# A recurrent step on four TensorE column tiles: seven equal x products a step instead of eight unequal ones, and a VectorE wait moved to a memset

## The chip, the cores and the metric

The kernel runs on one core of a Trainium2 chip. The metric is the device time of one execution in microseconds. Before the change the median of three runs is 1675.38 us (1673.64 to 1677.71).

## The reference, cut to what matters

Eight sequences of 512 steps and 512 features go through a gated recurrent cell with 512 units; the result is added to the input.

```python
def step(h, x_t):
    fused = sigmoid(concat([x_t, h], -1) @ w_W + w_b)
    hidden_state, output_state = split(fused, 2, -1)          # r and z
    memory_state = x_t @ wx_W + wx_b + hidden_state * (h @ wh_W + wh_b)
    h_new = output_state * h + (1 - output_state) * tanh(memory_state)
    return h_new, h_new
# x: (8, 512, 512) float32; out = x + all h_new
```

A step needs h times three 512 x 512 matrices (for r, for z and for hh, the product that r scales), and x times three. The x part does not depend on the state and can be worked ahead. Everything is float32.

## The kernel before

**Layout.** The state lies with its units on the partitions, in four chunks of 128 (k = 0 to 3). Chunks 0 and 1 are half A (tiles `hTA`), 2 and 3 half B (`hTB`). A matmul takes a chunk of the state as its stationary operand: 32 columns wide, four time steps by eight sequences, of which the current step's eight count. The moving operand is a block of weights. The array is used as four column tiles of 32 columns; tile j (j = 0 to 3) writes PSUM partitions 32j to 32j+31, and each tile has its own quarter of the weights. A float32 matmul is two weight loads and two matmul records in the profile.

**The h products of a step.** They go to three PSUM tiles: `A`, 192 columns (hh, z and r of half A), `B`, 128 (r and hh of half B) and `C`, 64 (z of half B), two of each in turn. `ORDER` (line 27) gives their order: A0 B0 A1 A2 A3 B1 B2 B3 C0 C1 C2 C3, letter and chunk; each entry is four matmuls, one per column tile, j = 0, 1, 2, 3. So the new state of half A is needed first, at A0, that of half B at A2.

**The x products.** They are worked for two groups of four steps at once, in a scheme with seven products where a plain one has eight: `products(o)` (line 289) yields their matmuls one by one, each product with two chunks k and four tiles j, on sums of weights (`tw`, lines 267 to 276) and sums of inputs (`sx`, made on GpSimd by `x_sum`). They add into four regions of two PSUM tiles `xp` (`AL`, `BE`, `GA`, `DE`, lines 35 and 36). ScalarE and VectorE copy and add these regions between steps (lines 463 to 501), at fixed places in a group of eight steps, and `spread` (line 247) puts the results into A, B and C as starting values of a later step. Of the 14 pairs of a product and a chunk in `products`, two are cut in two halves of 96 columns, so that eight steps have 64 matmuls. After each step's h products `take(later, 8)` (line 355) issues the next eight. This holds from step 5 on; the steps before take them from `first`, and the last ones have none left.

**The elementwise chain of a step.** The order is written out by hand (line 180 turns the scheduler off, and each engine works its instructions in program order). VectorE transposes r of half A from PSUM (`tr`, line 377), then hh of half A (`md1A`, line 393), then z (`tz`). ScalarE takes the sigmoids (`act`, line 214). A VectorE scan (`scan`, line 361) computes r times hh plus the x part into `m`, ScalarE takes tanh, and a second scan (`update`) makes the new state. The two scans of a half run chunk by chunk. Half B follows in the same way between half A's instructions. The scan into `m` reads md1A, which VectorE has written itself, and md0A, which ScalarE has written; line 403 makes tz of half A, which stands before the scan, wait for md1A's transpose.

**The step's end.** After the copies, three memsets of one column of the tile `idle` (line 506) stand on VectorE ahead of the next step's tr. GpSimd adds the input to the state for the output, and SyncE stores 16 steps at a time.

Of the kernel before, what the change touches and what calls it, by code (L numbers as in the profile page):

```python
# [14 lines left out]
NQ = 4  # L15
# [7 lines left out]
IDLE = 3  # L23
# [9 lines left out]
HALF = 192  # L33
# [8 lines left out]
def tile_cond_rnn_residual(  # L42
# [39 lines left out]
    nc = tc.nc  # L82
# [51 lines left out]
    def wh(bank, k, j):  # L134
        return wa[:, k, j] if bank == "A" else wb[:, k, j, {"C": slice(0, 64), "B": slice(64, 192)}[bank]]
# [30 lines left out]
    idle = const.tile([P, IDLE], F32, name="idle")  # L166
# [8 lines left out]
    def state(hf, i, slot=2):  # L175

        s = i % GS
        return hT[hf][i % NH][:, B * s : B * s + B, :, slot]
# [8 lines left out]
    def mm(out_, lhsT, rhs, start=False):  # L187
        nc.tensor.matmul(  # L188
            out_, lhsT, rhs, start=start, stop=False, skip_group_check=True
        )  # L190
# [13 lines left out]
    for hf in range(2):  # L204
        for slot in (0, 2):
            nc.vector.tensor_copy(
                state(hf, 0, slot), hin[:, 2 * hf : 2 * hf + 2].rearrange("p c b -> p b c")
            )

# [2 lines left out]
    def act(key, out_, in_, func, **kw):  # L214
        inst = nc.scalar.activation(out_, in_, func, **kw).ins  # L215
        if key in written:
            tc.declare_no_dep(inst, written[key], reason="ordered through VectorE")
        written[key] = inst
        return inst
# [37 lines left out]
    def reg(r):  # L257
        return xps[r[0]][:, r[1]]

    def wx_of(kh, ch):  # L260
        return wx[:, 2 * kh : 2 * kh + 2, :, HALF * ch : HALF * ch + HALF]

    def x_half(o, n, kh):

        return x_of(o // 2, slice(2 * kh, 2 * kh + 2), 8 * (o % 2) + GS * n, GS)
# [23 lines left out]
    def products(o):  # L289

        t_ = [q[o % 2] for q in sx]
        for n, (to, lhs, rhs) in enumerate((
            (AL, x_half(o, 0, 0), wx_of(0, 0)),
            (DE, t_[0], tw[0]),
            (BE, t_[1], tw[1]),
            (AL, x_half(o, 0, 1), wx_of(1, 0)),
            (GA, t_[2], tw[2]),
            (BE, t_[3], wx_of(1, 1)),
            (GA, x_half(o, 1, 1), tw[3]),
        )):  # L300
            for k in range(2):
                w = HALF // 2 if (2 * n + k) % 7 == 3 else HALF
                for c0 in range(0, HALF, w):
                    for j in range(NQ):
                        mm(
                            reg(to)[32 * j : 32 * j + 32, c0 : c0 + w],
                            lhs[:, k],
                            rhs[:, k, j, c0 : c0 + w],
                        )
                        yield  # L310

    def take(it, n=None):
        while n is None or n > 0:
            if next(it, it) is it:
                return
            n = None if n is None else n - 1

    def x_side():
        for o in range(2, NG // 2):
            yield from products(o)  # L320
# [4 lines left out]
    later = x_side()  # L325
# [8 lines left out]
    for i in range(T):  # L334
# [8 lines left out]
        for n in (ORDER if i else FIRST).split():  # L343
            if n == "x":
                take(first[1], 1)
                continue
            bank, k = n[0], int(n[1])
            hs = hT[k // 2][i % NH][:, :, k % 2, 2]
            for j in range(NQ):
                to = ps[bank] if i or bank != "A" else xps[0][:, XP["A"]]  # L350
                mm(to[32 * j : 32 * j + 32, :], hs, wh(bank, k, j))
        if i < 5:
            take(first[(i + 3) // 2], 2)
        else:
            take(later, 8)

        rows = slice(B * s, B * s + B)

# [16 lines left out]
        def turned(n, hf):  # L375
            t_ = work.tile([P, 2, 32], F32, tag=f"t{n}{hf}", name=f"t{n}{hf}_{i}")
            inst = nc.vector.transpose(t_.rearrange("p c n -> p (c n)"), raw[n][hf]).ins  # L377
            return t_[:, :, rows], inst
# [19 lines left out]
                tc.add_manual_dep(inst, pool_done[i + 1 - NH].name, SYNC)  # L398

        def turn_z(hf):  # L400
            tz, inst = turned("z", hf)
            if hf == 0:
                tc.add_manual_dep(inst, h_done[0].name, SYNC)
            act(
                ("zc", hf, i % 2),
                hd0[hf][i % 2][:, :, :, 2].rearrange("p n c -> p c n"),
                tz,
                AF.Sigmoid,
                scale=-1.0,
            )  # L410
# [17 lines left out]
        turn_r(0)  # L428
        turn_h(0)
        turn_z(0)  # L430
        memory(0, 0)
        memory(0, 1)
        turn_r(1)
        turn_h(1)
        update(0, 0)
        turn_z(1)
        tc.add_manual_dep(update(0, 1), r_done[1].name, SYNC)
        if i == 0:
# [64 lines left out]
            weight_sum(1 if i < 5 else 3, *divmod((i - 1) % 4, 2))  # L503
        if i == 4:
            nc.gpsimd.tensor_tensor(step_bias, bias[:, BE[1]], bias[:, AL[1]], ALU.subtract)
        for n in range(IDLE):
            nc.vector.memset(idle[:, n : n + 1], 0.0)
        def add(hf, engine):
            return engine.tensor_tensor(  # L509
# [98 lines left out]
```

## Time and profile before

| | before |
|---|---|
| median of 3 runs | 1675.38 us (1673.64 to 1677.71) |
| profiled execution | 1671.65 us, span 1669.3 us |
| granted TensorE clock | 1.00 |
| busy PE | 1655.0 us (99%), 57230 matmul records |
| busy VectorE, ScalarE, GpSimd | 1102.7, 956.9, 300.5 us |
| DMA, mean over the span | 19 GB/s |

PE is TensorE's matmuls, PEld its weight loads, DVE VectorE, ACT ScalarE, POOL GpSimd, SP SyncE. In a group's row the numbers after the bar are busy time in us and the mean duration of one in ns; after the second bar stand the idle time of the engine before these instructions and what ended it. In a timeline row the first number is the start in us from the beginning of the span, the second the duration of the row's instructions together. In the list of waits the numbers are us in total, the number of waits and the sources. The span covers all 512 steps and a prologue.

### The profile page before, as it was taken

To read this page: it belongs to the slowest core of one execution; us is meant where nothing else is said; L and a number is where in the kernel's file an instruction comes from. 1 tells how busy PE (TensorE), PEld (TensorE's weight loads), DVE (VectorE), ACT (ScalarE), POOL (GpSimd) and SP (SyncE) were. 2 spreads that over 40 slices of the span, in tenths; PEclk is the share of its full clock that TensorE was granted. 3 is DMA by queue.
4 is the path that set the end of the run, shared out by engine and by line. 5 is a ranking of instruction groups with operands and counts; after the bars stand their busy time and mean duration, and the time that the engine had idled before them with its cause. 6 is when DMAs were issued, how large, how long until landed. Compare 5 with 4: busy or idle time off the path is not lost.

```text
span 1669.3 us, 131859 instructions
## 1 busy us (share of the span) xinstructions
PE 1655.0 (99%) x57230; PEld 1504.4 (90%) x57230; DVE 1102.7 (66%) x9387; ACT 956.9 (57%) x5822; POOL 300.5 (18%) x1281
## 2 busy tenths in 40 slices
PE   8999999999999999999999999999999999999998
PEld 5999999999999999999999989999899999999997
DVE  6666666666666666666666666666666666666666
ACT  3555555555555555555555555555555555555555
POOL 1111111111111111111111111111111111111111
PEclk9999999999999999999999999999999999999999
DMA  4000000000000000000000000000000000000000
GB/s 179 17 11 12 18 18 18 17 5 18 17 18 18 5 18 18 17 17 5 18 18 17 18 17 5 18 17 17 18 5 18 17 18 18 5 17 12 11 11 11
DMA packets 11533, 31.53 MB, mean 19 GB/s; under 512 B 1220, under 2 KB 1732, under 8 KB 10824
## 3 DMA queue, kind: packets, MB, share of 16 engines
q1 hardware_dynamic: 10800, 22.94, 3.9%
q8 instruction: 448, 7.34, 1.8%
q14 instruction: 133, 1.09, 0.2%
q10 hardware_dynamic: 152, 0.16, 0.0%
HBM read 14.70 MB, written 8.39 MB: 14 GB/s over the span
## 4 chain that ended last, share of the span: by engine, by line
PE 97%; DMA 1%; DVE 1%; issue 0%; ACT 0%; SPq 0%
PE A L188 40%; PE B L188 26%; PE xp L188 18%; PE C L188 13%; DMA wb<-in_wb_dram 1%; DMA wx<-in_wx_dram 0%; DVE tr L377 0%; DVE tz L377 0%; DVE hTA L361 0%; DVE m L361 0%; DVE md1A L393 0%; DVE md1B L393 0%; ACT hTB L215 0%; ACT xp L223 0%; DVE hTB L361 0%
## 5 line engine op out<-in xcount | busy, mean ns | idle before, releaser
L188 PE MATMUL A<-wa,hTA 128*32 128x192 f32 x8176 | 536.1, 328 | 2.8 <-DVE hTA L361 2.8
L188 PE MATMUL A<-wa,hTB 128*32 128x192 f32 x8176 | 435.6, 326 | 0.1
L188 PE MATMUL B<-wb,hTA 128*32 128x128 f32 x8192 | 429.5, 273 | 0.8 <-DMA wb<-in_wb_dram 0.8
L377 DVE STREAM_TRANSPOSE tr<-A 128x64 f32<-128x64 f32 x511 | 127.7, 250 | 435.6 <-PE A L188 435.6
L509 POOL TENSOR_TENSOR ot<-xin,hTB 128x16 f32<-128x16 f32 x503 | 125.5, 250 | 1324.8 <-DVE hTB L361 1314.1
L188 PEld LDWEIGHTS B<-wb,hTA 128*32 128x32 f32 x8192 | 307.5, 122 | 37.6 <-DMA wb<-in_wb_dram 1.1
L215 ACT ACTIVATE md0A<-tr 128x16 f32<-128x16 f32 x512 | 112.7, 220 | 397.6 <-DVE tr L377 397.6
L188 PEld LDWEIGHTS A<-wa,hTB 128*32 128x32 f32 x8176 | 292.3, 122 | 45.7 <-DVE hTB L361 0.7
L188 PE MATMUL B<-wb,hTB 128*32 128x128 f32 x8192 | 327.1, 273 | 0.1
L188 PEld LDWEIGHTS A<-wa,hTA 128*32 128x32 f32 x8176 | 263.9, 123 | 37.5 <-DVE hTA L361 22.4
L188 PEld LDWEIGHTS B<-wb,hTB 128*32 128x32 f32 x8192 | 249.6, 122 | 0.3 <-DMA wb<-in_wb_dram 0.3
L361 DVE TENSOR_TENSOR_SCAN hTB<-hd0B,hTB 128x24 f32<-128x24 f32 x1024 | 157.7, 195 | 100.5 <-ACT hTB L215 100.3
L188 PE MATMUL C<-wb,hTB 128*32 128x64 f32 x8192 | 218.6, 219 | 1.0 <-issue 1.0
L188 PE MATMUL C<-wb,hTA 128*32 128x64 f32 x8192 | 217.9, 219 | 0.0
L188 PEld LDWEIGHTS C<-wb,hTA 128*32 128x32 f32 x8192 | 195.4, 122 | 0.0
L361 DVE TENSOR_TENSOR_SCAN hTA<-hd0A,hTA 128x24 f32<-128x24 f32 x1024 | 191.0, 186 | 0.0
L188 PE MATMUL xp<-tw,sx 128*32 128x192 f32 (+1 forms) x3472 | 186.1, 303 | 0.3 <-issue 0.2
L215 ACT ACTIVATE hd0B<-tz 128x16 f32<-128x16 f32 x512 | 114.9, 224 | 110.7 <-DVE tz L377 110.7
L215 ACT ACTIVATE hd0A<-tz 128x16 f32<-128x16 f32 x512 | 115.1, 225 | 101.3 <-DVE tz L377 101.3
L188 PEld LDWEIGHTS C<-wb,hTB 128*32 128x32 f32 x8192 | 167.2, 122 | 0.9 <-issue 0.8
L215 ACT ACTIVATE hTB<-hTB 128x16 f32<-128x16 f32 x512 | 120.3, 235 | 78.7 <-DVE hTB L361 63.2
L215 ACT ACTIVATE hTB<-m 128x8 f32<-128x8 f32 x1024 | 160.6, 206 | 0.0
(91 smaller groups left out, 2281.5 us busy)
## 6 DMA issues: line engine op xcount, KB each, us to landing
xin<-in_x_dram SPq DMA_DIRECT2D x31, 256.0 KB, 3.0
out_dram<-ot SPq DMA_DIRECT2D x31, 256.0 KB, 2.2
wx<-in_wx_dram SPq DMA_DIRECT2D x4, 768.0 KB, 6.8
wa<-in_wa_dram SPq DMA_DIRECT2D x4, 384.0 KB, 8.8
wb<-in_wb_dram SPq DMA_DIRECT2D x1, 1152.0 KB
wb<-in_wb_dram SPq DMA_DIRECT2D x1, 384.0 KB, 11.2
out_dram<-ot SPq DMA_DIRECT2D x1, 192.0 KB, 1.9
head<-in_xh_dram ACTq DMA_DIRECT2D x1, 144.0 KB, 4.8
```

Of the source, the lines that this page charges most:

```text
L188: nc.tensor.matmul(out_, lhsT, rhs, start=start, stop=False, skip_group_check=True)
L215: inst = nc.scalar.activation(out_, in_, func, **kw).ins
L361: return nc.vector.tensor_tensor_scan(*[t_[:, :, c_].rearrange("p n c s -> p (n c s)") for t_ in (out_, d0, d1)], 0.0, ALU.mult, ALU.add,).ins
L377: inst = nc.vector.transpose(t_.rearrange("p c n -> p (c n)"), raw[n][hf]).ins
L509: return engine.tensor_tensor(ot[:, t, 2 * hf : 2 * hf + 2, :].rearrange("p c n -> p n c"), x_of(c, slice(2 * hf, 2 * hf + 2), t, 1).rearr ...
```

## The change

Two things change. First, `products` no longer cuts two pairs in halves: all matmuls have 192 columns, 56 of them per eight steps, and a step takes seven (`take(later, 7)`). Seven is not a multiple of four, so the column tiles are taken in turn: the variable `turn` counts the x matmuls issued, and the h products of a step begin at the tile at which the x products of the step before left off. Second, the wait for md1A's transpose of half A is taken from tz and put on a memset of the last column of `idle`, which now stands between md1A's transpose and tz in VectorE's program; the step's end has two memsets left.

```diff
@@ products(o)
-        for n, (to, lhs, rhs) in enumerate((
+        for to, lhs, rhs in (
 ...
             for k in range(2):
-                w = HALF // 2 if (2 * n + k) % 7 == 3 else HALF
-                for c0 in range(0, HALF, w):
-                    for j in range(NQ):
-                        mm(
-                            reg(to)[32 * j : 32 * j + 32, c0 : c0 + w],
-                            lhs[:, k],
-                            rhs[:, k, j, c0 : c0 + w],
-                        )
-                        yield
+                for j in range(NQ):
+                    mm(reg(to)[32 * j : 32 * j + 32], lhs[:, k], rhs[:, k, j])
+                    yield
@@ the step's h products (turn = [0] before the loop)
             for j in range(NQ):
+                j = (j + turn[0]) % NQ
                 to = ps[bank] if i or bank != "A" else xps[0][:, XP["A"]]
                 mm(to[32 * j : 32 * j + 32, :], hs, wh(bank, k, j))
         if i < 5:
             take(first[(i + 3) // 2], 2)
         else:
-            take(later, 8)
+            take(later, 7)
+            turn[0] += 7
@@ turn_z(hf)
-            tz, inst = turned("z", hf)
+            tz, _ = turned("z", hf)
             if hf == 0:
+                inst = nc.vector.memset(idle[:, IDLE - 1 :], 0.0).ins
                 tc.add_manual_dep(inst, h_done[0].name, SYNC)
@@ the step's end
-        for n in range(IDLE):
+        for n in range(IDLE - 1):
             nc.vector.memset(idle[:, n : n + 1], 0.0)
```

## The prediction

> **What bounds the kernel now.** I read the page's parts 1 and 4 first, then the list of waits, then the timeline step by step.
>
> ```profile
> PE 1655.0 (99%) x57230; PEld 1504.4 (90%) x57230; DVE 1102.7 (66%) x9387; ACT 956.9 (57%) x5822; POOL 300.5 (18%) x1281
> PE 97%; DMA 1%; DVE 1%; issue 0%; ACT 0%; SPq 0%
> PEld A L188 <- DVE hTA L361: 22.4, 119, 0.4
> ```
>
> TensorE is nearly the whole chain, and the only wait of the steady state that reaches it is its first weight load of a step (bank A, stationary hTA) waiting for VectorE's new state: 22.4 us, in 119 steps. A share cannot say which steps these are. The start of the transpose `tr<-A` marks each step once; here are three stretches of the VectorE timeline.
>
> ```profile
> 802.44 0.25 DVE L377 STREAM_TRANSPOSE tr<-A 128x64 f32<-128x64 f32 x1 [0.60 <-PE A L188]
> 805.56 0.25 DVE L377 STREAM_TRANSPOSE tr<-A 128x64 f32<-128x64 f32 x1 [0.59 <-PE A L188]
> 808.83 0.25 DVE L377 STREAM_TRANSPOSE tr<-A 128x64 f32<-128x64 f32 x1 [0.97 <-PE A L188]
> 812.10 0.25 DVE L377 STREAM_TRANSPOSE tr<-A 128x64 f32<-128x64 f32 x1 [0.97 <-PE A L188]
> 815.23 0.25 DVE L377 STREAM_TRANSPOSE tr<-A 128x64 f32<-128x64 f32 x1 [0.83 <-PE A L188]
> ...
> 1648.66 0.25 DVE L377 STREAM_TRANSPOSE tr<-A 128x64 f32<-128x64 f32 x1 [0.83 <-PE A L188]
> 1651.78 0.25 DVE L377 STREAM_TRANSPOSE tr<-A 128x64 f32<-128x64 f32 x1 [0.83 <-PE A L188]
> ```
>
> There are two kinds of step. After 805.56 come two of 3.27 us, then one of 3.13; over the whole trace the median by position in the group of eight is 3.270 four times and 3.126 four times, mean 3.198. The last ten steps have no x products at all and take 3.124 us (1648.66 to 1651.78). The TensorE timeline tells why.
>
> ```profile
> 803.29 0.67 PE L188 MATMUL xp<-wx,sx 128*32 128x96 f32 x16
> 803.78 0.52 PE L188 MATMUL A<-wa,hTA 128*32 128x192 f32 x8
> 806.41 0.83 PE L188 MATMUL xp<-tw,xin 128*32 128x192 f32 x16
> 807.06 0.51 PE L188 MATMUL A<-wa,hTA 128*32 128x192 f32 x8
> ```
>
> A matmul is two records (57230 for half as many calls). Eight x products of 192 columns hold TensorE from 806.41 to 807.06, 0.65 us, and since the four column tiles run side by side that is two products per tile at 0.325. Where four of the eight are halves it is 0.49 (803.29 to 803.78). So a tile's own h work is 3.27 - 0.65 = 2.62 us a step. A 3.27 step is filled by TensorE. A 3.126 step has 2.62 + 0.49 = 3.11 of work and is set by the loop through the state, which closes in 3.124 even with no x work: bank A done, transposes, sigmoid, tanh, update, next A.
>
> **Do the tiles depend on each other?** The change gives them unequal work, so this decides the sum. Now and then a disturbance puts two tiles ahead, as here:
>
> ```profile
> 564.03 0.33 PE L188 MATMUL C<-wb,hTB 128*32 128x64 f32 x8
> 564.14 0.34 PE L188 MATMUL xp<-wx,xin 128*32 128x192 f32 x2
> 564.19 0.28 PE L188 MATMUL C<-wb,hTB 128*32 128x64 f32 x4
> 564.30 0.50 PE L188 MATMUL xp<-wx,xin 128*32 128x192 f32 x6
> ```
>
> Two x matmuls begin at 564.14 while the other tiles still have C matmuls to begin at 564.19, though all C stand before all x in the program. Each tile runs through its own list, here 0.16 us ahead, and the steps around it are still 3.27 us. So a tile that is short of work does not shorten the others' lists. It runs ahead until it needs the next state, and that waits for bank A of the last tile.
>
> **The change, part by part: x products.** The seven products times two k times four tiles are 56 matmuls of 192 columns per eight steps either way; before, two of the 14 rounds were cut in halves to make 64. No column is removed. Per step it is now seven products: three tiles get two and one gets one, and since 7 = 2+2+2+1 and the order turns by seven, the short tile is another one each step.
>
> A tile with two products needs 2.62 + 0.65 = 3.27 us. The short one needs 2.62 + 0.325 = 2.945, but its next product needs the new state. That comes by the loop from the last tile's A. In the turned order the tile that is short now was the last one before, so the loop is counted from its own A: 3.124, less the 0.02 by which the fourth tile starts after the first in those steps (starts at 803.781 to 803.800), so 3.10. The trace agrees: in its disturbed stretches a lead kept over two full steps ends at 0.17 = 3.27 - 3.10. The short tile thus idles 0.16 us, and idle time on a tile cannot be lent to another.
>
> Every tile has the same four steps in turn: 3 x 3.27 + 3.10 = 12.91, or 3.2275 a step, with leads of 0.13, 0.085 and 0.04 between the tiles. Against 3.198 that is +0.029 us. The x products run in steps 5 to 500, 496 of them (7,936 records of 16 per step): **+14.4 us**. The 0.02 left aside, it would be 3.2335 and +17.6. The gain that even steps could have brought, 2.62 + 0.56 = 3.18 to 3.19, is 0.008 x 496 = 4 us.
>
> The trace's rows are at odds here with the Trainium skill, "TensorE: Matmul & The Clock Gate", Part 3, which has matmuls on packed tiles as "strict FIFO, no reordering", in start and in end. By it a lead could not exceed one pass (56 ns in C), the short tile would lose some 0.07 us more in four steps, and the sum would be, an estimate, +23 us. The rows at 564 show a lead of 0.16 that outlives C, and I go by them.
>
> Products now end a little earlier or later within their step, but ScalarE's copies and VectorE's sums that read them stay behind the same step's products, about 1 us later (the copy at L495 starts at 814.44, its step's x work ends at 813.44). Only the first product's last round moves, from step 5 to step 6 of a group of eight, still ahead of that copy. I cost this at nothing; a copy that waited would cost its own step only.
>
> **The memset.** The wait for md1A stands now on tz of half A:
>
> ```profile
> L377 DVE STREAM_TRANSPOSE tz<-A 128x64 f32<-128x64 f32 x511 | 127.9, 250 | 17.7
> L377 DVE STREAM_TRANSPOSE tz<-C 128x64 f32<-128x64 f32 x512 | 115.0, 225 | 1.3 <-PE C L188 1.2
> L507 DVE MEMSET idle<- 128x1 f32 x1536 | 38.8, 59 | 0.0
> ```
>
> tz is on the loop: the scan `m` starts 0.17 after it, and tanh stands behind tz's sigmoid on ScalarE. With the wait on a memset in front, all of VectorE's queue is still held (tz, two scans, then half B's transposes), so nothing passes. The memset adds at most its 59 ns; three in a row take 0.08, so about 8 each when they follow one another. A transposing that really waits takes 250 ns and one that need not takes 225 (tz<-C; tr<-B is 227), so 24 ns may be won. Bounds for the loop: -24 to +59; I take 8 - 24 = -16, since the memsets in a row are the nearest pair. Only the short tile's step feels it: a quarter in 496 steps, the whole in some eleven without x: -16 ns gives -2.2 us, the ends are -3.3 and +8.0. The memset gone from the step's end lay in VectorE's idle 0.6 to 0.97 us before tr and is worth nothing.
>
> **Sum.** The profiled execution took 1671.65 us (span 1669.3 and 2.35 around it): 1671.65 + 14.4 - 2.2 = 1683.9. The median of the three runs lies 3.7 above it, so **1687.5 us**. The mean step from 37.67 to 1633.04 was 3.2165, so 9 us lie in irregular long steps; I leave them as they are, give or take 3.
>
> **Rivals.** *Faster:* the short tile's idle closes and every step is 3.19: 1671.65 - 4 - 2 = 1665.7, median about 1669.5. It needs the loop at 2.945, 0.155 us shorter; to break even it needs 4 x 3.198 - 9.81 = 2.98, 0.12 below 3.10. The memset can give 0.024. Against it are also the 119 waits. 9%.
>
> *Much slower:* the round cannot be broken, because a waiting weight load holds the whole queue, and seven products cost two full rounds: every step is 3.27, +0.072 x 496 = +35.7, 1711. It decides if a lead is lost at the first load's wait in each step. For it: in a disturbed step three tiles begin nothing between 694.63 and 694.79, with no wait named. Against it: leads that outlived two or three steps of 3.27. 10%.
>
> *No change that can be measured* (0.2%, about 3.4 us, is what a measurement of this kernel can tell): leads never build up, and the short tile's loss halves with a shorter loop. 4%.
>
> **How the numbers follow.** My case has 77%. Its own range: down to 1687.5 - 1.1 (best memset) - 3 (long steps) - 2.5 (the runs' spread), 1681; up to 1687.5 + 10.2 (worst memset) + 3.2 (the 0.02) + 3, 1704. The two far rivals hold 19%, so the range can leave both out: 1681 to 1704. Faster 0.10 (the rival and a little more), same 0.04, slower 0.86.
>
> **What would show it.** In the changed profile the starts of tr<-A should be evenly spaced near 3.22 to 3.24 us; TensorE's four tiles should be apart by some 0.04 us each, with A, B or C records of two banks mixed; the wait of PEld A for hTA should turn up in nearly every x step (496, not 119); tz<-A should last about 225 ns, and the last ten steps tell the memset's price without the tiles: 3.11 if I am right, up to 3.18. Even steps of 3.19 with no such wait would prove me wrong, and so would 3.27 with tiles in line.

## The result and the profile after

The changed kernel takes 1673.15 us (median of 20 runs, 1671.52 to 1676.89). The kernel before, run beside it, takes 1676.95 (20 runs, 1671.76 to 1682.16). The ratio is 0.9979 with a 95% interval of 0.9971 to 0.9986: faster by 0.21%, just past what can be told apart. The forecast was 1687.5, with a range of 1681 to 1704. Both its sign and its range were wrong.

The profiled executions alone would mislead. Before took 1671.65 us and after 1673.31, so the traced run of after is the longer one. The trace of before is one of its quick executions, 5.3 us under its median of 20. Why before scatters more than after is the main finding below.

The page of after, parts 1, 3 and 4; the row of q8 gives packets, MB and share of the DMA engines:

```profile
span 1670.8 us, 129875 instructions
...
PE 1659.0 (99%) x56238; PEld 1637.5 (98%) x56238; DVE 1090.5 (65%) x9387; ACT 1029.9 (62%) x5822; POOL 301.9 (18%) x1281
...
q8 instruction: 440, 7.21, 1.8%
...
PE 98%; DVE 1%; DMA 0%; issue 0%; ACT 0%
```

TensorE is still the chain. It has 992 matmul records fewer, and PEld is busy for 98% of the span instead of 90%; that fits tiles which no longer load together. Two rows of the list of waits of after (us in total, number, and the longest single wait in us; the third number is not the sources, as the part ahead of the prediction has it):

```profile
PEld xp L188 <- issue: 8.0, 24, 0.7
PEld A L188 <- DVE hTA L358: 4.0, 11, 0.4
```

The wait for hTA fell from 119 steps to 11, where I had expected 496; ten of the 11 lie behind 1620 us, in the steps without x work at the end. The VectorE timeline of after, the start of every step in the stretch shown of before, and two of the last steps without x work:

```profile
802.27 0.25 DVE L374 STREAM_TRANSPOSE tr<-A 128x64 f32<-128x64 f32 x1 [1.02 <-PE A L188]
805.46 0.25 DVE L374 STREAM_TRANSPOSE tr<-A 128x64 f32<-128x64 f32 x1 [0.70 <-PE A L188]
808.71 0.25 DVE L374 STREAM_TRANSPOSE tr<-A 128x64 f32<-128x64 f32 x1 [0.77 <-PE A L188]
811.90 0.25 DVE L374 STREAM_TRANSPOSE tr<-A 128x64 f32<-128x64 f32 x1 [0.94 <-PE A L188]
815.13 0.25 DVE L374 STREAM_TRANSPOSE tr<-A 128x64 f32<-128x64 f32 x1 [0.98 <-PE A L188]
...
1647.36 0.25 DVE L374 STREAM_TRANSPOSE tr<-A 128x64 f32<-128x64 f32 x1 [0.83 <-PE A L188]
1650.44 0.25 DVE L374 STREAM_TRANSPOSE tr<-A 128x64 f32<-128x64 f32 x1 [0.84 <-PE A L188]
```

The two kinds of step are gone: the four steps take 3.19, 3.25, 3.19 and 3.23. The median by position in the group of eight lies between 3.209 and 3.216 everywhere, mean 3.211. A step without x work takes 3.08 instead of 3.124. TensorE's timeline of after shows what the tiles do at a step's end:

```profile
803.00 0.33 PE L188 MATMUL xp<-tw,sx 128*32 128x192 f32 x1
803.00 0.28 PE L188 MATMUL C<-wb,hTB 128*32 128x64 f32 x4
803.07 0.33 PE L188 MATMUL xp<-tw,sx 128*32 128x192 f32 x2
803.12 0.22 PE L188 MATMUL C<-wb,hTB 128*32 128x64 f32 x1
...
803.56 0.35 PE L188 MATMUL A<-wa,hTA 128*32 128x192 f32 x1
803.56 0.33 PE L188 MATMUL xp<-wx,sx 128*32 128x192 f32 x2
```

x matmuls start at 803.00 while a C matmul of another tile starts as late as 803.12, and the next step's first A starts beside x matmuls of the old one (803.56). The last four A records of a step start 0.162 us apart (median); before it was 0.020.

Last, VectorE's chain in a step of after, and its groups:

```profile
802.44 0.21 DVE L390 STREAM_TRANSPOSE md1A<-A 128x64 f32<-128x64 f32 x1
802.58 0.21 DVE L374 STREAM_TRANSPOSE tz<-A 128x64 f32<-128x64 f32 x1
802.74 0.06 DVE L400 MEMSET idle<- 128x1 f32 x1
802.81 0.28 DVE L358 TENSOR_TENSOR_SCAN m<-md0A,md1A 128x16 f32<-128x16 f32 x2
```

```profile
L374 DVE STREAM_TRANSPOSE tz<-A 128x64 f32<-128x64 f32 x511 | 105.9, 207 | 0.0
L400 DVE MEMSET idle<- 128x1 f32 x512 | 30.2, 59 | 0.0
```

The memset runs after tz, not ahead of it as both the change's description above and my prediction have it: `turned("z", hf)` issues the transpose, and the memset is written below that line. So tz waits for nothing, and when the memset starts md1A's transpose is over. tz starts 0.305 us after tr (0.417 before) and lasts 207 ns (250 before). `m` starts 0.535 after tr (0.591) and half A's update 1.011 (1.053). The loop is 44 ns shorter.

### The profile page after: what moved, and what is told of

Read it like the earlier page. It is cut to its first block, busy times and chain, and to the rows that moved or that the text cites. A ratio compares the mean times of both kernels' runs of the same rounds, so it can differ in the third digit from the quotient of the medians.

```text
span 1670.8 us, 129875 instructions
## 1 busy us (share of the span) xinstructions
PE 1659.0 (99%) x56238; PEld 1637.5 (98%) x56238; DVE 1090.5 (65%) x9387; ACT 1029.9 (62%) x5822; POOL 301.9 (18%) x1281
## 4 chain that ended last, share of the span: by engine, by line
PE 98%; DVE 1%; DMA 0%; issue 0%; ACT 0%
PE A L188 44%; PE B L188 23%; PE xp L188 20%; PE C L188 12%; DMA rows<-in_bias_dram 0%; DVE tr L374 0%; DVE m L358 0%; DVE tz L374 0%; DVE md1B L390 0%; DVE md1A L390 0%; DVE hTA L358 0%; DVE bias L203 0%; ACT hTB L216 0%; ACT xp L224 0%; DVE rows L120 0%
## 5 line engine op out<-in xcount | busy, mean ns | idle before, releaser
L188 PE MATMUL A<-wa,hTA 128*32 128x192 f32 x8176 | 638.2, 329 | 2.3 <-DVE hTA L358 2.3
L188 PE MATMUL B<-wb,hTA 128*32 128x128 f32 x8192 | 573.8, 273 | 0.0
L188 PE MATMUL A<-wa,hTB 128*32 128x192 f32 x8176 | 507.4, 326 | 0.5 <-DVE hTB L358 0.5
L188 PEld LDWEIGHTS B<-wb,hTA 128*32 128x32 f32 x8192 | 471.2, 122 | 1.4 <-issue 0.2
L188 PE MATMUL B<-wb,hTB 128*32 128x128 f32 x8192 | 398.9, 273 | 0.0
L188 PEld LDWEIGHTS A<-wa,hTA 128*32 128x32 f32 x8176 | 385.4, 123 | 7.6 <-DVE hTA L358 4.0
L188 PEld LDWEIGHTS A<-wa,hTB 128*32 128x32 f32 x8176 | 372.9, 122 | 2.7 <-DVE hTB L358 0.8
L188 PEld LDWEIGHTS B<-wb,hTB 128*32 128x32 f32 x8192 | 321.5, 122 | 0.1
L188 PE MATMUL xp<-tw,sx 128*32 128x192 f32 x2976 | 237.2, 326 | 0.1
L188 PE MATMUL xp<-wx,xin 128*32 128x192 f32 (+1 forms) x2048 | 182.4, 331 | 0.7 <-issue 0.5
```

The source lines that it names most:

```text
L188: nc.tensor.matmul(out_, lhsT, rhs, start=start, stop=False, skip_group_check=True)
```

## Where the time went

I split each trace into regular steps (steps 5 to 500 at the median of their position) and what the rest are longer by.

| us | before | after |
|---|---|---|
| profiled execution | 1671.65 | 1673.31 |
| excess of irregular steps | 9.1 | 4.1 |
| what is left | 1662.5 | 1669.2 |

So the regular work did become slower, by 6.7 us. The irregular steps became cheaper by 5.0 in these traces. (The median by position is a fair measure where the steps at one position are alike, as in these two traces; it is not in every experiment.) At the medians, if what is left is the same there, the excess is 1676.95 - 1662.5 = 14.4 before and 1673.15 - 1669.2 = 4.0 after: +6.7 - 10.4 = -3.8 us. (The 14.4 is a remainder; no trace of that run was taken.)

**What the irregular steps are.** The timelines of VectorE and of TensorE's weight loads, and the page of before, at one of them:

```profile
1207.08 0.25 DVE L377 STREAM_TRANSPOSE tr<-A 128x64 f32<-128x64 f32 x1 [0.97 <-PE A L188]
1211.11 0.25 DVE L377 STREAM_TRANSPOSE tr<-A 128x64 f32<-128x64 f32 x1 [1.74 <-PE A L188]
```

```profile
1208.67 0.16 PEld L188 LDWEIGHTS xp<-wx,xin 128*32 128x32 f32 x8 [0.71 <-ACT md0B L215]
```

```profile
q8 instruction: 448, 7.34, 1.8%
```

The step takes 4.03 us, because TensorE loads nothing for 0.71 us. The profile names a sigmoid of ScalarE, but the releaser is inferred, and this x load does not read that tile. Now count: before has 2 x 57230 = 114,460 TensorE records, divided by 256 that is 447.1, and queue 8 moved 448 packets of 7.34 MB / 448 = 16.4 KB. After: 112,476 / 256 = 439.4 and 440 packets. So TensorE's program comes in blocks of 256 instructions. I numbered the records of each trace in the order of their starts, the 226 semaphore and drain records of TensorE's queue included, and looked at every gap of more than 170 ns between two starts in steps 5 to 500. In before all 14 (5.4 us together) stand at number 193 modulo 256 (the first record is number 0), in after all 6 (2.5 us) at the same number. If a block begins at each such number, 448 begin in before and 440 in after, just as many as there are packets. Against the mean of all other gaps the starts of blocks cost 6.2 us in before and 2.3 in after, of excesses of 9.1 and 4.1; for the rest no place is shown.

The gap at 1208.67 is one of the 14. The last instruction packet ahead of it ran from 1206.11 to 1207.20, 1.47 us before the first record of the block; the median lead is 1.88 us in before and 2.03 in after, and in neither trace is a first record less than 1.19 us behind its packet. All 14 long gaps of before stand at blocks with a lead of 1.27 to 1.62 us (113 of 435 blocks have 1.62 or less, and none with more has a long gap), the 6 of after at 1.25 to 1.51. The reading that fits is that TensorE at times uses up a block before the next one is ready. A block lasts 3.70 us (median) in before and 3.80 in after: fewer matmul calls for the same columns leave more time for the fetch. That the number of calls is what counts is tested below.

## The experiments

They were run in several series, and the time of the kernel before itself varied from series to series (1672.3 to 1696.8). Each ratio is against the kernel before in the same series.

**The memset alone**

```diff
@@ before: turn_z(hf); the step's end: range(IDLE - 1)
+                inst = nc.vector.memset(idle[:, IDLE - 1 :], 0.0).ins
                 tc.add_manual_dep(inst, h_done[0].name, SYNC)
```

> The memset alone; x products as before. Theory (tiles set the clean step, and the change's gain comes from rarer long irregular steps once the tiles are out of step): the loop shortens from 3.124 to 3.080, so the light steps fall from 3.126 to their 3.11 of TensorE work and the mean regular step from 3.198 to 3.190: 4.0 us, and 0.5 in the steps without x. The irregular part stays as before's. Sum: 4.5 us faster than before. Rival (the shorter loop is what removes the irregular part, some 10 us of it): 14 us faster.

1666.39 us (10 runs) against 1672.3, ratio 0.9965 (0.9952 to 0.9978). Its VectorE timeline:

```profile
804.35 0.25 DVE L377 STREAM_TRANSPOSE tr<-A 128x64 f32<-128x64 f32 x1 [0.63 <-PE A L188]
807.62 0.25 DVE L377 STREAM_TRANSPOSE tr<-A 128x64 f32<-128x64 f32 x1 [1.02 <-PE A L188]
810.88 0.25 DVE L377 STREAM_TRANSPOSE tr<-A 128x64 f32<-128x64 f32 x1 [1.03 <-PE A L188]
814.00 0.25 DVE L377 STREAM_TRANSPOSE tr<-A 128x64 f32<-128x64 f32 x1 [0.86 <-PE A L188]
```

Steps of 3.27 and 3.11, mean 3.190. The loop is now 3.078, but a light step stops at 3.11, its own TensorE work. So half the steps gain 16 ns each (3.126 to 3.110), some 4 us; -5.9 was measured, where 4.5 were expected. The irregular steps are still there: 11.0 us of excess in its trace. It was not compared with after in one series, so whether it beats the full change stays open.

**The turned products alone**

```diff
@@ after: turn_z(hf); the step's end: range(IDLE)
-            tz, _ = turned("z", hf)
+            tz, inst = turned("z", hf)
             if hf == 0:
-                inst = nc.vector.memset(idle[:, IDLE - 1 :], 0.0).ins
```

> Seven products with the tiles in turn alone; the wait stays on tz. Theory: the short tile's loop is 3.124 - 0.021 - 0.029 = 3.074, so the regular step is (3.074 + 3 x 3.27)/4 = 3.221 against 3.198, +11.4 us, and the irregular part falls by some 10 us: about 1 us slower than before, between 2 faster and 4 slower. Rival (the irregular part falls through the shorter loop, so here it stays): 11 us slower.

1676.65 us (10 runs) against 1672.3, ratio 1.0024 (1.0015 to 1.0033): slower by 4.4 us, just outside the 2 faster to 4 slower that were expected. The regular steps are 3.230 by the medians, where 3.221 was expected; the mean with all irregular ones is 3.226, so here the medians are some ns too high. Both parts together beat before although this part alone loses. With unequal tiles the loop enters every step, so the memset's 44 ns should count in each of them by a quarter, 11 ns; by the medians it is 19 (3.230 to 3.211).

**Fewer calls without tiles apart**

```diff
@@ after
-            take(later, 7)
-            turn[0] += 7
+            take(later, 4 if (i - 5) % 4 == 3 else 8)
```

> The memset, and the seven products without halves and without turning: two whole rounds of four tiles in three steps, one in the fourth. As few TensorE instructions as in the changed kernel, but the tiles stay in step. Regular step (3 x 3.27 + 3.08)/4 = 3.2225, +12.1 us. Theory (tiles out of step make the long steps rarer): the irregular part stays, 11 to 12 us slower than before. Rival (fewer instructions make them rarer): about 2 us slower.

1676.74 us (8 runs) against 1672.3, ratio 1.0026 (1.0016 to 1.0036). The regular steps are three of 3.270 and one of 3.080, mean 3.222, as expected. The tiles are in step (0.020 us), and still the irregular excess is only 1.6 us, where the memset alone with the calls of before has 11.0. So the tiles need not be apart for it. It points to the number of calls, but the regular step is longer here too; the calls put back into after, below, exclude that rival. The total missed both numbers: +4.4, between the 2 and the 11 expected.

**Without x loads and stores, before and after**

```diff
@@ both kernels
-        if c < NCH:
+        if 4 <= c < NCH:
+            xins[c] = xins[c - 3]
+        elif c < 4:
@@ both: stores at the end of 16 steps
-        elif t == TC - 1:
-            store(0)
-            xins.pop(c)
```

> The kernel before without the loads of x from the fifth block of 16 steps on (blocks 1 to 3 are read again) and without the stores of the output but the last. Theory (the irregular long steps come from this traffic): the irregular part, 9 us in the profiled execution of before and some 14 in its median, nearly vanishes: 12 to 14 us faster than before, regular steps unchanged at 3.27 and 3.126. Rival (they have another origin): no faster.

> The changed kernel with the same traffic left out. Theory: only its irregular part of some 4 us vanishes, so it comes out about 6 us slower than the kernel before without the traffic, which is the price of the uneven tiles (regular step 3.211 against 3.198). Rival (the changed kernel's gain is in its regular steps): it keeps its lead of 4 us.

In a series in which the kernel before took 1696.8, before without the traffic took 1687.73 (6 runs; ratio 0.9944, 0.9924 to 0.9964), and after without it 1673.96 (5 runs; 0.9867, 0.9848 to 0.9886). Both expectations missed. The excess did not vanish from before: its trace still holds 25.9 us of it, after's 3.9. The traffic is only a part. In the first trace of before, 2.2 of the 9.1 us lay in the step after a block of x is loaded and a store goes out (one step of 16). Without traffic that step holds 1.1 of 25.9 us and no longer stands out.

**A slower loop by a pad**

```diff
@@ before and after: a pad of 128 columns
                 tc.add_manual_dep(inst, h_done[0].name, SYNC)
+                nc.vector.memset(pad, 0.0)
```

> The kernel before with one more VectorE memset of 128 columns between tz of half A and the scan into m, which makes the loop some 0.11 us longer. Theory: only the light steps feel it (3.126 to about 3.235; the 3.27 steps have 0.146 to spare): half of 496 steps, +27 us, and +1 in the last steps: 28 us slower than before.

> The changed kernel with the same memset of 128 columns. Theory (each tile has one short step in four and only that one runs through the loop): the regular step rises by a quarter of 0.11, 0.0275, +13.6 us and +1 in the last steps, about 15 us slower than the changed kernel. Rival (the uneven tiles make every step wait for the loop): +55 us. Rival (TensorE alone sets the step at 3.19 to 3.21): +1 us.

Before with the pad: 1702.76 us (12 runs) against 1696.8, ratio 1.0042 (1.0026 to 1.0059). Its update starts 87 ns later, light steps take 3.211 (+85 ns), heavy ones stay at 3.270, so the regular mean rose by 43 ns. That is 21 us (28 were expected), of which only 6 arrived. That the rest is less standing still is not shown: the trace of the padded kernel has an excess of 20.8 us, and I have no trace of the kernel before in this series. After with the pad: 1677.61 (6 runs; 0.9886, 0.9868 to 0.9904). Here the pad hid: `m`'s first scan started 50 ns later but ended 0.727 after tr as without the pad (142 ns instead of 192), and the update still started at 1.011. What else holds that scan is not shown: ScalarE's sigmoid is over at 0.503 in both traces. So this run tells nothing of the loop.

So the pad was doubled on after:

```diff
@@ after: a pad of 256 columns
                 tc.add_manual_dep(inst, h_done[0].name, SYNC)
+                nc.vector.memset(pad, 0.0)
```

> The changed kernel with a VectorE memset of 256 columns before the scan into m; one of 128 columns still hid behind the scan's wait for the sigmoid. The loop is 0.11 us longer (tr to the update 1.01 to 1.12). Theory (only the short tile's step runs through the loop): the regular step rises by a quarter of it, 3.211 to 3.239. Rival (every step waits for the loop): 3.32. Rival (TensorE alone): 3.211.

One execution (1686.84 us) and its trace. The update starts at 1.127 (+0.116), a step without x work takes 3.197, and the regular step 3.247, +36 ns for 116: a factor of 0.31 by the medians, and 0.20 by the mean of all steps (3.243 against 3.220), on both sides of the quarter that the tile model gives. That rules out the whole 116 and nothing.

**The calls put back into after**

> The changed kernel once more, as the measure for the others of this call on the same chip: regular step 3.211, irregular part some 4 us, median 1672 to 1675 whatever the kernel before takes on this chip.

The changed kernel again, in the series of the next: 1673.44 us (5 runs) against 1679.64, ratio 0.9964 (0.9949 to 0.9978); regular steps 3.213, excess 2.7 us.

```diff
@@ after: one of seven matmuls cut in two; in the second kernel "in (2, 5)" for "== 3"
-                    mm(reg(to)[32 * j : 32 * j + 32], lhs[:, k], rhs[:, k, j])
+                    w = HALF // 2 if cut[0] % 7 == 3 else HALF
+                    for c0 in range(0, HALF, w):
+                        mm(reg(to)[32 * j : 32 * j + 32, c0 : c0 + w], lhs[:, k], rhs[:, k, j, c0 : c0 + w])
+                    cut[0] += 1
```

> The changed kernel with one of the seven products of each step cut into two halves of 96 columns on the same tile: the same columns and the same turning order, but 64 TensorE calls in eight steps for x where there were 56. Theory (the long steps are waits for TensorE's next block of 256 instructions, and come more often when a block is used up faster): the regular step stays at 3.21, and the irregular part returns to before's 9 us or more: 5 to 12 us slower than the changed kernel. Rival (tiles out of step make them rarer): no more than 1 us slower.

1681.32 us (12 runs) against the same 1679.64, ratio 1.0012 (0.9997 to 1.0027): 7.9 us over the uncut kernel. The regular step is the same (3.214), the excess is 10.0 us instead of 2.7. So 64 calls for 56, with the columns, the turning order and the regular step as they were, cost 7.9 us (5 to 12 were expected), and the irregular steps of the two traces differ by 7.3.

> The changed kernel with two of the seven products of each step cut into halves: 72 calls for x in eight steps, where one cut gave 64 and the changed kernel has 56. With 64 calls, eight steps are 1,792 TensorE records, just seven blocks of 256, so that a block begins at the same places of the group again and again; with 72 they are 1,824 and with 56 they are 1,760, and the places move. Theory (a block that is used up faster comes due before its successor is there): the irregular part is larger still than with one cut, 10 us or more, and the time 2 to 10 us above that kernel's. Rival (the standing alignment of blocks and steps makes the long steps): the irregular part falls back to 2 to 5 us, as in the changed kernel, and the time is 1673 to 1676.

72 calls in eight steps: 1713.56 us (5 runs) against 1687.16 in this series, ratio 1.0154 (1.0139 to 1.0168). From its page, and from its list of waits:

```profile
PE 1690.7 (99%) x58222; PEld 1650.2 (96%) x58222; DVE 1096.7 (64%) x9387; ACT 1029.8 (60%) x5822; POOL 301.9 (18%) x1281
...
q8 instruction: 455, 7.45, 1.8%
```

```profile
PEld xp L188 <- issue: 12.4, 44, 0.6
PEld C L188 <- issue: 10.3, 30, 0.7
```

Here the profile says "issue": the engine waits for nothing that the profile shows. All 77 gaps over 170 ns (26.8 us) stand at number 193 modulo 256, and the excess is 26.3 us. But the median step is not the same either: it rose to 3.248 from the 3.214 with 64 calls, so the excess over it is not the whole loss. Against the mean of all other gaps the starts of blocks cost 30.8 us, 7.3 with 64 calls. The two kernels' times differ by 32 us, in different series, where 2 to 10 were expected; some 9 of the 32 have no place in this account. The rival, that a step's calls must not line up with the blocks, foretold no such loss: 72 calls make 1,824 records in eight steps, which is not a multiple of 256. But a block lasts 3.71 us here, no less than in before, where the excess is 9.1: the median length of a block alone does not give the size of the loss.

**Fewer calls still: B and C in one PSUM tile**

```diff
@@ before with the memset
-ORDER = "A0 B0 A1 A2 A3 B1 B2 B3 C0 C1 C2 C3"
+ORDER = "A0 B0 A1 A2 A3 D1 B2 B3 C0 C2 C3"
 ...
-BANKS = {"A": 192, "B": 128, "C": 64}
+BANKS = {"A": 192, "D": 192}
 ... (B and C become slices of D, its weights 192 columns)
```

> The memset alone (x products in halves, tiles in step, regular step 3.190) with B and C of chunk 1 merged into one matmul of 192 columns, for which B and C share a PSUM tile: the same columns, 4 TensorE calls less in each step (52 where there were 56, fewer than the 55 of the changed kernel). Theory (instruction supply): the irregular part falls below the changed kernel's 4 us, at a regular step of 3.185 to 3.190: 10 to 13 us faster than the changed kernel. Rival (tiles out of step are what counts): the irregular part stays at 11 us or more and the kernel is no faster than with the memset alone.

1782.88 us (4 runs) against 1679.64, ratio 1.0616 (1.06 to 1.0632). Its list of waits:

```profile
PEld A L188 <- DVE hTA L364: 185.4, 507, 0.7
...
DVE tr L380 <- PE D L188: 145.4, 512, 1.8
```

Half B's transpose now waits until the C products into the shared tile are done too, in every step, and each step takes 3.431. As an improvement it fails (10 to 13 us faster than the changed kernel were expected). But its blocks last 4.30 us and their packets lead by 2.68, and its irregular excess is nil (-0.04 us).

## Why the prediction was wrong

- **"9 us lie in irregular long steps; I leave them as they are, give or take 3."** This is the step that failed, and it costs the sign. The excess fell to 4. In the sum I carried 9.1 plus the 3.7 between the trace and the median, 12.8; measured are some 4.0: 8.8 of the 14.3 us by which the forecast missed. I counted matmul columns ("no column is removed") and took calls to be free. The front page of the profile had the count: 57230 records, 448 packets.
- **"+14.4 us" for the x products.** Right in kind, and not shown to be wrong in size. The steps are even, the tiles are apart, the regular work is slower. The turned products alone have regular steps of 3.230 by the medians and 3.226 by the mean; over 3.198 that is +16 or +14 us.
- **"-16" for the memset, "in front" of tz.** I misread the program. Behind tz it is worth 44 ns, outside my bounds of -24 to +59, since I had bounded another arrangement. This is the second term that was mis-sized: -2.2 us in the sum, where a quarter of 44 ns in 496 steps is -5.5, and the medians with and without it (3.211 and 3.230) give -9. The two regular terms together were to give +12.2; measured are +6.7.
- **The short tile's loop.** With 3.03 in place of 3.10 the same formula gives (3.03 + 3 x 3.27) / 4 = 3.21, and 3.211 was measured. Of the 0.07, 44 ns come from the memset. For the other 30 I have a time that I had taken as fixed: from the start of the last A record to tr it is 393 ns when four tiles end together and 363 when the last ends alone. That this shortens the step is not shown: it is 363 in the turned products alone too, where the formula with it gave 3.221 and 3.230 was measured.
- **"496, not 119" waits for hTA.** 11 were seen. The list counts time in which no weight load runs at all, and the other three tiles load while the short one idles. That is a view of the engine and not of a tile.
- **Rivals.** "Faster", at 9%, came true in its sign and not in its mechanism: its even 3.19 was not reached (3.211), nor its loop of 2.98 (3.03 by the formula above). "Much slower" asked for 3.27 with tiles in line; the tiles are 0.162 apart. For it I had cited 694.63 to 694.79, where "three tiles begin nothing, with no wait named"; the record that ends that stop, at 694.80, is the first of a block (number 193 modulo 256). Such stops were the clue to the standing still, and I used them only for that rival.

On one point the trace had been the better guide. The Trainium skill, "TensorE: Matmul & The Clock Gate", Part 3, has matmuls on packed tiles as strict FIFO; the rows of after at 803.00 to 803.12, with x started beside older C, differ from it, as do nearly all steps of after, and the measurement decides.

**What stays open.** It is not shown what sets off the fetch of the next block; ahead of the 14 long gaps of before the packet started 1.20 us after the block before had begun, ahead of the other blocks 0.70 (medians). Nor is it shown why the fetch would be late more often in some series than in others (the experiments ran on three chips, but one chip alone had 1672.3 and 1679.64), or why the loss with 72 calls is as large as it is. So it is open how far the gain of 0.21% carries: it was 0.36% (ratio 0.9964) in the second comparison. A version with the 3.190 of the first experiment and fewer calls was not found; the one tried for it failed by the shared tile.

## What to carry to other kernels

Where TensorE is 99% busy with short matmuls, the number of its instructions is a cost of its own: count its records per packet of the instruction queue (256 here), take the time of a block, and look whether long gaps stand at one number modulo the block. Fewer and wider matmuls can then win even though they make the regular step longer. And split a time into regular steps and the rest before forecasting; the rest is a term with a cause, not a constant.

## What the runs showed of the hardware

- TensorE's program comes in blocks of 256 instructions (16.4 KB), and TensorE can stand still at the start of one: 14 gaps over 170 ns in the trace of before (3.70 us a block), 6 in after (3.80), 77 with 72 calls (3.71). In all fourteen traces a block's first record comes 1.19 us or more after the end of the last packet ahead of it; the shortest is between 1.19 and 1.28 in every kernel but the merged one (1.84).
- The time varies between series with the same program: the kernel before ran at 1672.3 to 1696.8 (medians).
- Column tiles keep their lead across PSUM tiles: in after x starts at 803.00 beside C until 803.12, and the last four A records start 0.162 us apart (median).
- A VectorE transpose that waits for the one in front takes 250 ns, one that need not 207; a one-column memset that carries the wait instead, behind tz, lasts 59, as the memsets at the step's end do in before.
